# A graph attention layer on one core: the targets in 128 rows, the weights behind the first stores, and the one-hot in the middle of the step

## The chip, the cores and the metric

The kernel is one program on one core of a Trainium2 chip. The core has five instruction queues that run beside each other: TensorE (PE in the profile; matrix products and transposes, results into PSUM), VectorE (DVE), ScalarE (ACT), GpSimd (POOL, here only the indirect gathers) and SyncE (SP, which here issues nearly all other transfers). Each queue works in order. Transfers run on sixteen DMA engines. The metric is the device time of one execution in microseconds (us).

## The reference

There are 12,500 nodes with 128 values each and 400,000 edges, which are sorted by their target node `dst`; `src` is any node. H is 8 heads of 16 values.

```python
h = maximum(layernorm(x), 0)
message = (h @ w_src + b_src)[src] + (h @ w_dst)[dst]
rad_w = silu(silu(edge_attr @ fc_w1 + fc_b1) @ fc_w2 + fc_b2) @ fc_w3 + fc_b3
message = message * edge_weight * rad_w
message = message @ w_sep + b_sep            # per head: 16 for alpha, 16 values
alpha = smooth_leaky_relu(message_alpha)
score = sum over 16 of alpha * alpha_dot
att = softmax of score over the edges with the same dst
out = sum over the edges with the same dst of value * att
return x + out @ w_proj + b_proj
```

## The kernel before, in words

The program has four stages, and in all of them the order of each queue is the order in which the lines are written.

**The node stage** (L152 to L341). `x` is loaded in seven groups of 14 blocks of 128 nodes and a tail (L162, L163). A loop over 25 quads of four blocks computes: `stats` (L214, VectorE, every second quad for eight blocks, with one `rstd` on ScalarE), `norm` (L226, ScalarE), `turn` (L234, TensorE transposes, VectorE copies to `hT`) and `products` (L246): products with both node weights into PSUM, copies to `ms` (four buffers; ScalarE, in every fourth quad one of them VectorE) and two stores to the tables `t_src` and `t_dst` (L266) on SP. Before the loop SP is given, in this order: x, the targets `dst` as `cur` in 125 rows of 3200 (L169), the same shifted by one place as `prev` (L171, L172), each pair's first targets for the two halves of a pair as `base` (L176), the sections' first and last targets as `ends` (L177), and the block forms `w1b`, `w2b`, `w3b`, `b12` of the radial weights (L188 to L194). ScalarE's queue is given the two node weights (L159, L160) and fifteen weight loads (`load`, L108, L110). Eight completion counters are shared by the transfers of SP and ScalarE in turn, so a transfer is issued when the eighth before it has landed.

Two jobs sit in or behind the loop. `fits` (L271, after quad 12) counts places where `prev > cur` and sections whose targets span 64 nodes or more; the count `bad` decides later between the window form, which is taken with these inputs, and a general form. It also stores `ends` and loads them again, spread over the partitions, as `eb`. `cuts` (L303, after the loop) makes `sm`, which marks where a target changes (two passes over 3200 columns on VectorE), and stores it as `same`; it derives `w_score`, `w_s`, `v_out`, `b_s` and the window starts `far` and `tgt`.

**The edge stage** (`windows`, L656). 400 pairs of sections of 500 edges; step k of the loop at L1027 works on pair k, and with a lag of 12 on the sums of pair c = k - 12. `step` (L948) fixes the order of the queues. SP in a step: the stores of the last sums (`store_win` L920, `store` L924, the latter with a start read from `base`), the loads for pair k+3 (`load_w` L713, `load_md` L719, in every second step `load_d` L707), for k+6 (`load_e` L702), and now and then others (`prep_load`, `load_sm`, `load_x` L931, `zero` L136, scores out and back L836, L841, maxima L870). GpSimd gathers the source rows `gs` (L739). TensorE: third layer of the radial net (`mlp3`, L790), source rows and target rows into `pm` (L803, L811), first half of the values (`values(c, 0)`, L901), first `pa` (`alphas(k, 0)`, L820), `mlp1` of k+2, second half of the values, more source rows, second `pa`, `mlp2`, then `sums(c)` (L912), which multiplies the weighted values `pvx` by a one-hot matrix `oh` of the targets.

VectorE's order in a step: `sums_begin(c)` (L880) makes `oh` with two instructions (L888, L891) after ScalarE has copied the softmax weights into `pvx` (L884); then two `rad` (L794), two `mT` (L816), the first `pvx` (L903), `mr` (L728), the first `al` (L824), the second `pvx`, the second `al`, `ohT` (L783), `m` (L732). In each group of eight steps the softmax of the group before adds two scans (L852, L857), a difference (L862), an Exp and a transpose; in 25 of these groups `add_x` (L938) adds a bias to a loaded block of x, and every sixteenth step prepares indices (`prep_make`, L683). Twelve further steps (L1158) end the sums, beside jobs that combine sections which share a node. **The last stage** divides, multiplies by `w_proj` and adds x.

Of the kernel before, what the change touches and what calls it, by code (L numbers as in the profile page):

```python
# [21 lines left out]
F32 = mybir.dt.float32  # L22
BF16 = mybir.dt.bfloat16
I32 = mybir.dt.int32
AF = mybir.ActivationFunctionType
ALU = mybir.AluOpType
AX = mybir.AxisListType
# [3 lines left out]
P = 128  # L31
C = 128
H = 8
RAD = 32
BANK = 512
FC = 64
# [4 lines left out]
RP = 125  # L41
# [6 lines left out]
SEC = T * TS  # L48
# [8 lines left out]
def gnn_kernel(ctx: ExitStack, tc: tile.TileContext, a: dict, out: bass.AP):  # L57
    nc = tc.nc
    x, src, dst = a["x"], a["src"], a["dst"]
    ea, ew = a["edge_attr_32"], a["edge_weight1"]  # L60
    N, E = x.shape[0], src.shape[0]
    NB = -(-N // P)
    NT = E // P
    RC = E // RP
    NS = E // SEC
# [6 lines left out]
    const = ctx.enter_context(tc.tile_pool(name="const", bufs=1))  # L72
# [10 lines left out]
    same = dram.tile([1, E + 1], BF16, name="same")  # L83
# [21 lines left out]
    ident = const.tile([P, P], F32, name="ident")  # L105
    make_identity(nc, ident)

    def load(name, shape, ap=None, eng=None):  # L108
        t = const.tile(shape, F32, name="c_" + name)
        (eng or nc.scalar).dma_start(out=t, in_=a[name] if ap is None else ap)  # L110
        return t

    eps = const.tile([P, 1], F32, name="eps")
    nc.vector.memset(eps, LN_EPS)
    ones = const.tile([P, P], F32, name="ones")
# [14 lines left out]
    base = const.tile([1, 2, NP], I32, name="base")  # L130
# [23 lines left out]
    with tc.tile_pool(name="node", bufs=2) as np_, tc.tile_pool(name="node1", bufs=1) as n1, \  # L154
# [6 lines left out]
        for t0, t1 in groups:  # L161
            nc.sync.dma_start(out=x_all[:, t0:t1, :], in_=x_v[:, t0:t1, :])  # L162
        nc.sync.dma_start(out=x_all[:tail, NF, :], in_=x[NF * P:, :])  # L163
        dst_r = dst.rearrange("(p c) -> p c", p=RP)
        cur = n1.tile([RP, RC], I32, name="cur")
        prev = n1.tile([RP, RC], I32, name="prev")
        ends = n1.tile([100, 8, 2], I32, name="ends")
        eb = n1.tile([P, NS, 2], I32, name="eb")
        nc.sync.dma_start(out=cur, in_=dst_r)  # L169
        nc.vector.memset(prev[0:1, 0:1], -1)  # L170
        nc.sync.dma_start(out=prev[0:1, 1:RC], in_=dst_r[0:1, 0:RC - 1])  # L171
        nc.sync.dma_start(out=prev[1:RP, :], in_=dst[RC - 1:E - 1].rearrange("(p c) -> p c", c=RC))  # L172
        at = dst[0:1]
        with nc.allow_non_contiguous_dma(reason="the sections' ends"):
            for f in range(2):
                nc.sync.dma_start(out=base[:, f, :], in_=dst_h[f:f + 1, :, 0])  # L176
            nc.sync.dma_start(out=ends, in_=bass.AP(  # L177
                at.tensor, at.offset, [[8 * SEC, 100], [SEC, 8], [SEC - 1, 2]]))

        w1b = const.tile([P, P], F32, name="w1b")  # L180
        nc.vector.memset(w1b, 0.0)
        w2b = const.tile([P, P], F32, name="w2b")
        w3b = const.tile([P, C], F32, name="w3b")
        b12 = const.tile([P, 2], F32, name="b12")
        for f in range(2):
            for q in range(2):
                o = (2 * q + f) * RAD
                nc.sync.dma_start(out=w1b[o:o + RAD, f * FC:(f + 1) * FC], in_=a["fc_w1"])  # L188
            s = slice(f * FC, (f + 1) * FC)
            for q in range(2):  # L190
                nc.sync.dma_start(out=w2b[s, q * FC:(q + 1) * FC], in_=a["fc_w2"])
            nc.sync.dma_start(out=w3b[s, :], in_=a["fc_w3"])
            nc.sync.dma_start(out=b12[s, 0:1], in_=a["fc_b1"])
            nc.sync.dma_start(out=b12[s, 1:2], in_=a["fc_b2"])  # L194
        b_n = load("b_n", [C, 1], a["b_src"].rearrange("o c -> c o"))
        dot = load("dot", [C, 1])
        heads = load("heads", [C, C])
        w1, b1 = load("fc_w1", [RAD, FC]), load("fc_b1", [FC, 1])
        w2, b2 = load("fc_w2", [FC, FC]), load("fc_b2", [FC, 1])
        w3, b3 = load("fc_w3", [FC, C]), load("fc_b3", [C, 1])  # L200
        w_a, b_a = load("w_a", [C, C]), load("b_a", [C, 1])
        w_v = load("w_v", [C, C])
        w_proj = load("w_proj", [C, C])
        b_out = load("b_out", [P, C], a["b_proj"].to_broadcast([P, C]))
        b_v = load("b_v", [C, 1])


        mv = n1.tile([P, NB, 2], F32, name="mv")
# [60 lines left out]


        def fits():  # L271
            gt = n1.tile([RP, RC], BF16, name="gt")
            nc.vector.tensor_tensor(gt, prev, cur, op=ALU.is_gt)
            cnt = n1.tile([P, 2], F32, name="cnt")
            nc.vector.memset(cnt, 0.0)
            nc.vector.tensor_reduce(cnt[:RP, 0:1], gt, AX.X, ALU.add)
            span = n1.tile([100, 8], F32, name="span")
            nc.vector.tensor_sub(span, ends[:, :, 1], ends[:, :, 0])
            nc.vector.tensor_scalar(span, span, float(W - 1), None, op0=ALU.is_ge)
            nc.vector.tensor_reduce(cnt[:100, 1:2], span, AX.X, ALU.add)  # L280
            tot = nps.tile([1, 1], F32, name="tot", bufs=1)
            for j in range(2):
                nc.tensor.matmul(tot, cnt[:, j:j + 1], ones[:, 0:1], start=(j == 0), stop=(j == 1))
            nc.vector.tensor_copy(bad, tot)
            nc.sync.dma_start(out=ends_d[:, 1:2 * NS + 1].rearrange("o (p c) -> (o p) c", p=100),
                              in_=ends.rearrange("p s i -> p (s i)"))
            none = n1.tile([1, 2], I32, name="none")
            nc.vector.memset(none, -1)
            nc.sync.dma_start(out=ends_d[:, 0:1], in_=none[:, 0:1])
            nc.sync.dma_start(out=ends_d[:, 2 * NS + 1:2 * NS + 2], in_=none[:, 1:2])  # L290
            nc.sync.dma_start(out=t_dst[N:N + W, :], in_=z[:W, 0:C])
            nc.sync.dma_start(out=eb.rearrange("p s i -> p (s i)"),
                              in_=ends_d[0:1, 1:2 * NS + 1].to_broadcast([P, 2 * NS]))
# [7 lines left out]
        v_out = const.tile([P, C], F32, name="v_out")  # L301

        def cuts():  # L303
            sm = n1.tile([RP, RC], BF16, name="sm")
            nc.vector.tensor_tensor(sm, prev, cur, op=ALU.not_equal)
            nc.vector.tensor_scalar(sm, sm, RESTART, None, op0=ALU.mult)
            nc.sync.dma_start(out=same[:, 0:E].rearrange("o (p c) -> (o p) c", p=RP), in_=sm)
            nc.sync.dma_start(out=same[:, E:E + 1], in_=sm[0:1, 0:1])
            nc.vector.tensor_scalar(w_score, heads, dot, 0.8, op0=ALU.mult, op1=ALU.mult)
            nc.vector.memset(w_s, 0.0)  # L310
# [21 lines left out]
        for i in range(Q):  # L332
            if i % 2 == 0 and 4 * i + G < NB:
                stats(4 * i + G, min(4 * i + 2 * G, NB))
            if i + 2 < Q:
                norm(i + 2)
            if i + 1 < Q:
                turn(i + 1)
            products(i)
            if i == 12:  # L340
                fits()  # L341
        cuts()


    chunks = [(t, min(CH, TPI - t)) for t in range(0, TPI, CH)]
# [310 lines left out]
    def windows():  # L656
# [5 lines left out]
        with tc.tile_pool(name="wk2", bufs=2) as sp, tc.tile_pool(name="ps", bufs=1, space=PSUM) as pp, \  # L662
# [214 lines left out]
                nc.scalar.copy(Pem[m].rearrange("p t q h -> p t (q h)"), pt)  # L877


            def sums_begin(c):  # L880
                pvx[c] = sp.tile([T, 2, TS, ROW], F32, name="pvx")
                q = c % MP * 2
                for f in range(2):
                    nc.scalar.copy(pvx[c][:, f, :, C:ROW], Pem[c // MP][:, :, q + f, :])  # L884
                _, loc = prep[c // 16]
                ohs[c] = sp.tile([T, 8, W], F32, name="oh")
                t0 = c % 16 * 8
# [60 lines left out]
            def step(k):  # L948
# [28 lines left out]
                if has(k + 1):  # L977
                    split_md(k + 1, 0)
                if has(c):
                    sums_begin(c)  # L980
                rad = mlp3(k) if has(k) else None
                if has(k):
                    sources(k, 1)
# [13 lines left out]
                    mlp1(k + 2)  # L997
                if has(c):
                    values(c, 1)

                if has(k + 1):
                    sources(k + 1, 0)
# [323 lines left out]
```

## Time and profile before

| what | value |
|---|---|
| median of 3 runs | 4723.23 us (4720.04 to 4723.61) |
| the profiled execution | 4712.63 us, its span 4710.8 us |
| mean granted TensorE clock | 0.964 |
| busy PE / DVE / ACT / POOL | 4212.0 / 3081.2 / 1921.9 / 3136.0 us |
| node stage, until the edge stage's first load | 155.00 us |
| edge loop, about | 165 to 4505 us |
| last twelve steps, and last stage | to 4627, and to the end |

Line numbers (L820) are those of the kernel. In a timeline each line gives start, duration, engine (SPq and ACTq are the queues when they issue a transfer), line, operation, output and inputs, form and, in brackets, how long the engine had been idle and what ended that. A line of waits gives who waited for what: total us, times, longest. Every duration comes from one profiled execution; the sums of the prediction are made against it and then set beside the median.

### The profile page before, as it was taken

The numbers are of one execution on the slowest core, as the hardware profiler recorded it, in microseconds if no ns is written. First come the engines' busy times: TensorE is split into PE (matmuls) and PEld (weight loads), VectorE is DVE, ScalarE is ACT, GpSimd is POOL, SyncE is SP. The second block draws the span as 40 slices with busy tenths as digits, with TensorE's granted clock in tenths as the row PEclk, the third lists the DMA queues.
The fourth block names the chain that finished last, engine by engine and source line by source line (L and its number), as shares of the span: only waits on it lengthen the run. The fifth ranks groups of instructions, "written<-read, shape, count | busy, mean of one in ns | idle before, by whom it ended". The sixth has DMA issues, their size and how long they took to land.

```text
span 4710.8 us, 88096 instructions
## 1 busy us (share of the span) xinstructions
PE 4212.0 (89%) x29692; PEld 2344.1 (50%) x29692; DVE 3081.2 (65%) x6005; ACT 1921.9 (41%) x4595; POOL 3136.0 (67%) x3223
## 2 busy tenths in 40 slices
PE   4669998999999999999999999999999999999974
PEld 3325554554555555555545555555555555555553
DVE  4436665766766666666666666666666666666666
ACT  3324443443443444443433444444444444444421
POOL 0467776776777777777766777777777767777601
PEclk8779999999999999999999999999999999999987
DMA  4667767777776777777777777777677777777724
GB/s 160 168 162 173 175 167 172 174 178 175 170 176 171 169 176 175 172 178 174 170 175 170 177 174 169 179 172 164 171 174 169 171 168 170 172 168 174 173 64 173
DMA packets 901312, 796.36 MB, mean 169 GB/s; under 512 B 530125, under 2 KB 776829, under 8 KB 900598
## 3 DMA queue, kind: packets, MB, share of 16 engines
q1 hardware_dynamic: 794830, 573.36, 46.8%
q0 software_dynamic: 102816, 210.37, 21.5%
q10 hardware_dynamic: 3202, 6.92, 0.4%
q8 instruction: 234, 3.83, 0.4%
q14 instruction: 230, 1.88, 0.1%
HBM read 649.99 MB, written 140.67 MB: 168 GB/s over the span
## 4 chain that ended last, share of the span: by engine, by line
PE 66%; DVE 10%; DMA 9%; SPq 6%; ACT 5%; issue 4%; POOL 1%; ACTq 0%; POOLq 0%; DVEq 0%
PE pa L820 14%; PE V L901 13%; PE misc L912 7%; PE p L790 6%; PE pm L803 6%; PE pm L811 4%; PE p L758 4%; PE misc L831 4%; PE p L773 4%; DMA md<-t_dst 2%; DMA sc_d<-Sp 2%; PE m L749 2%; ACT sl L822 2%; DMA agg<-ob 2%; DVE al L824 2%
## 5 line engine op out<-in xcount | busy, mean ns | idle before, releaser
L739 POOL DMA_INDIRECT gs<-t_src,idx x3200 | 3121.6, 976 | 1347.2 <-issue 800.8
L822 ACT ACTIVATE sl<-pa,c_b_a 128x500 f32<-128x500 f32 x800 | 541.4, 677 | 1595.5 <-PE pa L820 1594.7
L824 DVE SCALAR_TENSOR_TENSOR al<-pa,sl 128x500 f32<-128x500 f32 x800 | 543.1, 679 | 828.8 <-ACT sl L822 723.6
L820 PE MATMUL pa<-mT,c_w_a 128*128 128x500 f32 x1600 | 851.2, 614 | 244.2 <-DVE mT L816 173.3
L901 PE MATMUL V<-c_w_v,mT 128*125 128x128 f32 x6208 | 895.5, 288 | 0.3
L901 PEld LDWEIGHTS V<-c_w_v,mT 128*125 128x125 f32 x6208 | 746.4, 190 | 290.7 <-issue 176.8
L794 DVE SCALAR_TENSOR_TENSOR rad<-p,c_fc_b,w_b 128x500 f32<-128x500 f32 x800 | 552.9, 733 | 307.2 <-PE p L790 305.7
L903 DVE TENSOR_TENSOR pvx<-V,Pem 125x512 f32<-125x512 f32 x776 | 531.9, 685 | 114.4 <-PE V L901 107.8
L816 DVE SCALAR_TENSOR_TENSOR mT<-pm,c_b_n,rad 128x500 f32<-128x500 f32 x800 | 552.5, 733 | 6.5 <-PE pm L811 6.5
L803 PEld LDWEIGHTS pm<-ident,gs 125*128 125x128 f32 x3200 | 356.7, 142 | 312.8 <-issue 292.3
L803 PE MATMUL pm<-ident,gs 125*128 125x125 f32 x3200 | 505.0, 280 | 7.9 <-DMA gs<-t_src,idx 7.9
L912 PE MATMUL misc<-pvx,oh 125*64 125x136 f32 x6400 | 470.1, 288 | 31.4 <-DVE pvx L903 27.6
L912 PEld LDWEIGHTS misc<-pvx,oh 125*64 125x64 f32 x6400 | 364.5, 138 | 182.9 <-issue 178.6
L790 PE MATMUL p<-h,w3b 64*128 64x500 f32 x1600 | 446.0, 634 | 2.4 <-ACT h L776 2.4
L820 PEld LDWEIGHTS pa<-mT,c_w_a 128*128 128x128 f32 x1600 | 245.0, 193 | 284.5 <-DVE mT L816 195.4
L811 PE MATMUL pm<-ohT,m 64*128 64x500 bf16 x2400 | 323.9, 376 | 0.0
L758 PE MATMUL p<-eT,w1b 64*128 64x250 f32 x1600 | 287.5, 437 | 1.0 <-ACT eT L751 1.0
L725 ACT CAST m<-md 128x128 bf16<-128x128 f32 x400 | 118.3, 296 | 401.1 <-DMA md<-t_dst 400.8
L758 PEld LDWEIGHTS p<-eT,w1b 64*128 64x128 f32 x1600 | 124.7, 191 | 307.5 <-issue 276.3
L761 ACT ACTIVATE h<-p,b 128x500 f32<-128x500 f32 x400 | 272.4, 681 | 4.8 <-PE p L758 4.8
L776 ACT ACTIVATE h<-p,b 128x500 f32<-128x500 f32 x400 | 269.2, 673 | 3.6 <-PE p L773 3.6
L888 DVE TENSOR_TENSOR oh<-lane,loc 125x504 f32<-125x504 f32 x400 | 269.2, 673 | 0.0
(145 smaller groups left out, 3286.1 us busy)
## 6 DMA issues: line engine op xcount, KB each, us to landing
w_b<-in_edge_weight SPq DMA_DIRECT2D x400, 500.0 KB
d_b<-in_dst SPq DMA_DIRECT2D x400, 250.0 KB
gs<-t_src,idx POOLq DMA_INDIRECT x3200
e_t<-in_edge_attr SPq DMA_DIRECT2D x400, 125.0 KB
sc_d<-Sp SPq DMA_DIRECT2D x200, 250.0 KB
win<-ob SPq DMA_DIRECT2D x400, 68.0 KB
agg<-ob SPq DMA_DIRECT2D x800, 33.5 KB
md<-t_dst SPq DMA_DIRECT2D x800, 32.0 KB
```

The lines of the kernel that those rows point to most:

```text
L739: nc.gpsimd.indirect_dma_start(out=gs[:, j, :], out_offset=None, in_=t_src[:, :], in_offset=bass.IndirectOffsetOnAxis(ap=idx[:, t:t + 1], ...
L758: nc.tensor.matmul(p1[:, q, 0:2 * T], w1b[s, :], eTs[k][s, :], start=True, stop=True)
L790: nc.tensor.matmul(p3[:, f, 0:SEC], w3b[s, :], h2s[k][s, :], start=True, stop=True)
L794: nc.vector.scalar_tensor_tensor(rad[:, s], p3[:, f, 0:SEC], b3, w_g[k][:, s], op0=ALU.add, op1=ALU.mult)
L803: nc.tensor.matmul(pms[k, f][:, t * T:(t + 1) * T], gs[:T, t, :], ident[:T, :T], start=(t == 0), stop=False, is_transpose=True, skip_group ...
L816: nc.vector.scalar_tensor_tensor(mTs[k][:, s], pm[f], b_n, rad[:, s], op0=ALU.add, op1=ALU.mult)
L820: nc.tensor.matmul(pa, w_a, mTs[k][:, f * SEC:(f + 1) * SEC], start=True, stop=True)
L822: nc.scalar.activation(sl, pa, AF.Silu, bias=b_a, scale=1.0)
L824: nc.vector.scalar_tensor_tensor(al, pa, 0.25, sl, op0=ALU.mult, op1=ALU.add)
L901: nc.tensor.matmul(V[:, t, :], mTs[c][:, o:o + T], w_v, start=True, stop=True)
L903: nc.vector.tensor_mul(pvx[c][:, f, :, 0:C].rearrange("p t (h k) -> p t h k", h=H), V.rearrange("p t (h k) -> p t h k", h=H), Pem[c // MP] ...
L912: nc.tensor.matmul(acc[f * W:(f + 1) * W, :], ohs[c][:, f * TS + t, :], pvx[c][:, f, t, :], start=(t == 0), stop=(t == TS - 1), skip_group ...
```

## The change

The separate loads on ScalarE's queue go. All weights and the targets are asked for on SP, after the stores of the second quad's products: first the targets, then the fifteen weights, then the block forms w1b, w2b, w3b and b12 in the order of before. The targets come once, as 128 rows of 3125 with one more column in front, whose value is the last target of the row before: `cur[:, 1:]` is what `cur` was, `cur[:, :-1]` what `prev` was. `cuts` runs after quad 20, inside the loop. In the edge stage `sums_begin` is cut in two: `weights(c)` stays at its place, and `one_hot(c)` is called after the second half of the values. All else is as before.

```diff
-    def load(name, shape, ap=None, eng=None):
-        t = const.tile(shape, F32, name="c_" + name)
-        (eng or nc.scalar).dma_start(out=t, in_=a[name] if ap is None else ap)
-        return t
...
-        nc.sync.dma_start(out=cur, in_=dst_r)
-        nc.vector.memset(prev[0:1, 0:1], -1)
-        nc.sync.dma_start(out=prev[0:1, 1:RC], in_=dst_r[0:1, 0:RC - 1])
-        nc.sync.dma_start(out=prev[1:RP, :], in_=dst[RC - 1:E - 1].rearrange("(p c) -> p c", c=RC))
...
+        CC = E // P
+        cur = n1.tile([P, CC + 1], I32, name="cur")
+        nc.vector.memset(cur[0:1, 0:1], -1)
...
+        wt = {name: const.tile(shape, F32, name="c_" + name) for name, shape in (
+            ("b_src", [C, 1]), ("dot", [C, 1]), ("heads", [C, C]), ("fc_w1", [RAD, FC]), ("fc_b1", [FC, 1]),
+            ("fc_w2", [FC, FC]), ("fc_b2", [FC, 1]), ("fc_w3", [FC, C]), ("fc_b3", [C, 1]), ("w_a", [C, C]),
+            ("b_a", [C, 1]), ("w_v", [C, C]), ("w_proj", [C, C]), ("b_proj", [P, C]), ("b_v", [C, 1]))}
...
+        def load_targets():
+            nc.sync.dma_start(out=cur[:, 1:CC + 1], in_=dst.rearrange("(p c) -> p c", p=P))
+            at = dst[CC - 1:CC]
+            with nc.allow_non_contiguous_dma(reason="single targets"):
+                nc.sync.dma_start(out=cur[1:P, 0:1], in_=bass.AP(at.tensor, at.offset, [[CC, P - 1], [1, 1]]))
+                for f in range(2):
+                    nc.sync.dma_start(out=base[:, f, :], in_=dst_h[f:f + 1, :, 0])
+                at = dst[0:1]
+                nc.sync.dma_start(out=ends, in_=bass.AP(
+                    at.tensor, at.offset, [[8 * SEC, 100], [SEC, 8], [SEC - 1, 2]]))
+
+        def load_weights():
+            for name, t in wt.items():
+                ap = a[name]
...
+                nc.sync.dma_start(out=t, in_=ap)
+            for f in range(2):
...
...
-            nc.vector.tensor_tensor(gt, prev, cur, op=ALU.is_gt)
+            nc.vector.tensor_tensor(gt, cur[:, 0:CC], cur[:, 1:CC + 1], op=ALU.is_gt)
...
-            nc.vector.tensor_tensor(sm, prev, cur, op=ALU.not_equal)
+            nc.vector.tensor_tensor(sm, cur[:, 0:CC], cur[:, 1:CC + 1], op=ALU.not_equal)
...
             products(i)
+            if i == 1:
+                load_targets()
+                load_weights()
             if i == 12:
                 fits()
-        cuts()
+            if i == 20:
+                cuts()
...
-            def sums_begin(c):
+            def weights(c):
                 pvx[c] = sp.tile([T, 2, TS, ROW], F32, name="pvx")
                 q = c % MP * 2
                 for f in range(2):
                     nc.scalar.copy(pvx[c][:, f, :, C:ROW], Pem[c // MP][:, :, q + f, :])
+
+            def one_hot(c):
                 _, loc = prep[c // 16]
                 ohs[c] = sp.tile([T, 8, W], F32, name="oh")
...
                 if has(c):
-                    sums_begin(c)
+                    weights(c)
...
                 if has(c):
                     values(c, 1)
+                    one_hot(c)
```

## The prediction

> **What bounds the kernel now.** I read the chain of waits first, then the waits in total, then the timeline of the start, of the end of the node stage and of steady steps, and last the SP queue's own waits.
>
> ```profile
> PE 66%; DVE 10%; DMA 9%; SPq 6%; ACT 5%; issue 4%; POOL 1%; ACTq 0%; POOLq 0%; DVEq 0%
> ```
>
> By the chain this looks like a TensorE kernel. It is one only inside a step. The start (all times in us from the span's start, columns start and duration):
>
> ```profile
> 14.53 1.28 ACT L221 ACT_TABLE_LOAD   x1 [14.53 <-DMA c_b_a<-in_b_a]
> 15.83 0.30 ACT L221 ACTIVATE rstd<-mv,eps 128x4 f32<-128x4 f32 x1
> ...
> 19.81 13.10 SPq L176 DMA_DIRECT2D base<-in_dst  x2
> 32.95 13.82 SPq L177 DMA_DIRECT2D ends<-in_dst  x1
> 46.89 15.71 SPq L188 DMA_DIRECT2D w1b<-in_fc_w  x2
> ...
> 70.05 0.52 SPq L266 DMA_DIRECT2D t_src<-ms  x1
> 73.29 0.58 ACT L261 COPY ms<-pm 128x512 f32<-128x512 f32 x1 [34.57 <-DMA t_dst<-ms]
> ```
>
> Two delays stand here. ScalarE cannot begin before 14.53, because its own queue issues fifteen weight loads until 14.50; the statistics of the first four blocks were ready at 7.79 (first BN_STATS 6.10, last aggregate 7.61 and 0.18). And the SP queue stands in three issues from 19.81 to 62, so the first store of node products leaves at 70.05; the four `ms` buffers are full, and ScalarE waits 34.57. What the queue stands behind is in the stretches (last two columns: share of the 16 DMA engines, GB/s):
>
> ```profile
> 20.00:25.00 5.00, 4.89 (x14) 3.24 (x14) 4.07 (x18) 2.40 (x7) 0.00 (x0) 1.00 1.01 422
> 30.00:35.00 5.00, 3.96 (x18) 2.84 (x19) 3.26 (x14) 4.73 (x12) 0.00 (x0) 1.00 0.34 123
> 50.00:55.00 5.00, 0.00 (x0) 0.00 (x0) 0.00 (x0) 0.00 (x0) 0.00 (x0) 0.50 0.24 85
> ```
>
> While x arrives all engines work; once only `cur` (125 rows) and `prev` (124) are left, a third to a quarter of them do. The node stage ends so:
>
> ```profile
> 142.19 3.48 DVE L305 TENSOR_TENSOR sm<-prev,cur 125x3200 bf16<-125x3200 int32 x1
> 147.07 0.28 SPq L307 DMA_DIRECT2D same<-sm  x1
> 155.00 0.36 SPq L674 DMA_DIRECT2D ri<-in_src  x1
> ```
>
> In the edge steps, one in eight looks like this:
>
> ```profile
> 2322.59 1.19 DVE L857 TENSOR_TENSOR_SCAN M<-sm,M 128x500 f32<-128x500 bf16 x1
> 2324.41 0.68 DVE L888 TENSOR_TENSOR oh<-lane,loc 125x504 f32<-125x504 f32 x1
> 2325.01 0.17 DVE L891 TENSOR_TENSOR oh<-loc,far 125x8 f32<-125x8 f32 x1
> 2325.09 1.38 DVE L794 SCALAR_TENSOR_TENSOR rad<-p,c_fc_b,w_b 128x500 f32<-128x500 f32 x2
> 2327.16 1.11 PE L820 MATMUL pa<-mT,c_w_a 128*128 128x500 f32 x2 [1.12 <-DVE mT L816]
> ```
>
> The scan makes VectorE late, the one-hot (L888, L891) stands before `rad`, and TensorE waits 1.12. But who paces the steps? The waits in total (us, times, longest):
>
> ```profile
> ACT m L725 <- DMA md<-t_dst: 400.8, 133, 10.6
> PE pa L820 <- DVE mT L816: 173.3, 93, 10.0
> DVE xs L938 <- DMA xs<-in_x: 74.9, 17, 9.7
> ```
>
> ```profile
> SPq L924 <- DMA agg<-ob: 150.8, 230, 7.8
> SPq L841 <- DMA sc_d<-Sp: 139.8, 49, 9.2
> ```
>
> The engines wait for what SP asked for late, while SP waits for its own transfers. I matched SP's issues with what they need, between 200 and 4480: each store of sums (L920) starts at least 2.5 after the copy (L916) that feeds it, median 12.1; each L836 at least 1.4 after its L834; each `w_b` load 11.4 or more after its buffer was last read. So SP never waits for a compute engine there; its issues follow each other without end. `md` is cast within 3.2 of its issue, with ScalarE idle, in 74 steps, the last at step 395 of 400. **The SP queue sets the length of the edge loop**; TensorE catches up with it and waits.
>
> **The change, part by part.**
>
> *ScalarE's queue loses the weight loads.* Only the two `w_nodes` remain, so the first `rstd` comes at 7.79 and some 0.06 instead of 15.83: 8.0 earlier, and all that follows it, up to the second products. x is no obstacle: it drains at 422 GB/s, and its second group is due only at 19.39 - 8.0 = 11.4.
>
> *The SP hold.* In the order of before without a stall, the second products are copied until 28.07; their two stores take to 29.05, now 21.05. Then the queue holds for a time H: five target loads, 29 weight loads. Those fifteen from ScalarE: 0.33 to 0.69 each in the trace with the gaps, without waits 8.2. The fourteen block loads: 62.19 to 69.94 for thirteen, so 8.3. The targets: `cur` 0.3, its transfer 1.6 MB at 422 GB/s is 3.8, behind half a MB of stores (1.3). The 127-row column has no row in the trace. Against the row of 128 single words that does stand there (`rb`, L680: issue 0.64, read 1.83 after it) it would cost 0.6. The Trainium skill, "DMA: Bandwidth & Descriptors", section "Why a DMA increments its semaphore by 16 and not by 1", speaks for one half of this edit and against the other: a transfer uses the largest number of engines up to 16 that divides its slow dimension, so 125 rows 5, 124 rows 4, 128 rows 16, but 127 rows one. The 0.34 and 0.24 above agree with 5 and 4 of 16 (0.31, 0.25). By it all 127 words queue on one engine behind its part of `cur`, and the two `base` loads cannot be accepted until most of them are taken, as L176 and L177 were not. I take this: 5.1 for `cur` and the stores, 1 for the column, 2 for `base` and `ends` (1600 words). That is 8.1; by the `rb` row alone it would be some 3, and as long as in before (2.5 + 10.5 + 13.8 of issue) 27. H = 8.1 + 8.2 + 8.3 = 24.6, bounds 19 and 43.
>
> Behind the hold stand the stores of products 2 to 5. `ms` has four buffers, so products 6 are the first to wait. Stores to the copy took 3.25 in before (70.05 to 73.29, rounded): the copy comes at 21.05 + 24.6 + 3.25 = 48.9. In before the copies of products 6 came at 80.21, and 74.8 later, at 155.00, the edge stage began. So 123.7, less 0.15 as the two passes of `fits` (3.48 and 3.49) shrink by 75 of 3200 columns.
>
> *The cuts in the middle.* Before, their VectorE work ran from 142.19 to 150.53, with `same` landing at 154.86 as the last thing (125 rows). The node stores alone had landed by 148.4 (the next stage's waits for them pass then), so 6.4 goes. But some 7.9 of VectorE work (the 8.3, less the shorter rows and part of a wait of 0.89 for TensorE) now stand ahead of the transposed copies of quad 22. The nearest row is `fits`, alike in form: with 7.8 of VectorE work the `rstd` that should come 6.81 after 98.25 came 14.57 after, 7.76 lost. Cost 7.8 - 6.4 = +1.4. If TensorE covers none of the gap before hT (0.96), less; bounds 0 and +3.5. In the upper one stands the scaling of `sm` (0.99 for 3200, a quarter of the 3.48 that one element per clock takes): rows are now 3125 long. By the row it is 0.97; one per clock would be 3.4. The Trainium skill, "VectorE: DVE Perf Modes", section "Walkthrough: the 8-slice pipeline in each mode", allows the fast form for an odd dimension if source and destination are equal, as they are here; no row shows it. I take 0.97. The two `same` issues cost SP 0.6 between stores, which then wait for VectorE anyway.
>
> Edge stage from 125.0 instead of 155.0: **-30**. GpSimd's gathers start with it and keep their distance; nothing is moved past its queue.
>
> *The one-hot.* Moved behind the second value product, before the second `al`. There VectorE waits 1.35 for ScalarE in an ordinary step (2018.47), the pair takes 0.60 and 0.17: hidden, and `oh` ends 1.36 after the second `pvx` begins (2006.10), 2007.46, before the sums begin at 2007.84. If the cover were gone, 388 x 0.77 = 299. At the old place it frees 0.68 in the steps where VectorE is late: over all steps, the smaller of what `rad` could come earlier and of TensorE's wait before `pa` adds up to 54. That is TensorE's time, not SP's: SP issues exactly as before, so what TensorE gains there it waits for `md` and `xs` later. Value 0 to -54; I take -0.5, what is left after step 395. In the twelve last steps nothing lies between pvx and the sums: three of them run TensorE, VectorE, TensorE in turn and get 0.95 each, the rest are held by other VectorE work or transfers: +3 (0 to +6).
>
> Sum: -30 + 3 - 0.5 = -27.5. The profiled run took 4712.6 around a span of 4710.8; the median of the runs is 4723.2. 4723.2 - 27.5 = **4696**.
>
> **The rivals.**
> *TensorE is the bound after all* (chain: 66%): the 54 arrive too, 4642. For it: TensorE is busy 4021 of 4340 in the loop. Against it: SP's issues never waited for it. 0.13, parts of it included.
> *The queue holds on as before*: the column on one engine blocks, H = 43, a stall of 30 instead of 11.5: 4715. For it: three issues of 10 to 15 in before. Against: those stood behind 33 us of transfers on 5 engines. 0.15.
> *Slower: the sums wait for the one-hot.* At L912, 16 matmuls in every step. The margin is 0.38; TensorE has some 0.7 per step to spare against SP (199 of idle on `md`, 75 on `xs`, over 400). So it decides from 1.1 late, and each 0.1 beyond costs 39: 1.25 late gives 4762. Against it: VectorE's idle time is there in nearly all steps (721 waits before `al`). 0.09.
>
> **How the numbers follow.** Forecast 0.63, with its own range 4684 to 4707 from the bounds of H, cuts and tail. The range 4650 to 4718 takes in parts of the first rival and most of the second; it leaves out about 0.2. A measurement of this kernel tells 0.2% (9.4) from nothing. Faster, below 4714: the forecast, the first rival and some of the second, 0.82; same 0.08; slower 0.10, the third rival and rest.
>
> **What would show it.** First `rstd` near 7.9; `cur` landing within 8 of its issue, the column's followers short; first store of products 2 near 46; edge stage from 125; one-hot without TensorE waiting at L912 in the loop; TensorE's wait for mT down by about 50 and ScalarE's wait for `md` up by the same; the loop from first to last step as long as before. Wrong would be a loop shorter by tens of us (SP not the pacer), or a hold over 40.

## The result, and the profile after

The changed kernel takes 4686.7 us (median of 5 runs, 4672.0 to 4692.86) where the kernel before takes 4721.15 (5 runs, 4716.71 to 4723.61): ratio 0.9923, 95% interval 0.9905 to 0.9941, so 28 to 45 us faster. On a second chip, in the run e9_changed below, it is 4601.4 against 4628.78: 0.9941, interval 0.9927 to 0.9956. Ratios and intervals leave out executions more than 1.5% above the fastest of the same kernel; only e12 had any (two of six). The two profiled executions differ by 25.9, and this is where:

| stretch of the profiled execution, us | before | after | difference |
|---|---|---|---|
| start, to the edge stage's first load | 155.00 | 123.00 | -32.00 |
| from there to the first `al` | 22.51 | 25.07 | +2.55 |
| edge loop, first `al` of its first step to first `al` of its last | 4331.48 | 4333.26 | +1.78 |
| from there to the end | 201.77 | 203.59 | +1.82 |
| span | 4710.77 | 4684.91 | -25.85 |

All the gain lies ahead of the edge stage; 2.55 of it is lost again on the way to the first `al`. The runs of one kernel lie up to 21 us apart, so the small differences behind it say no more than "unchanged".

The chain of waits on the page of the changed kernel (shares of the span by engine):

```profile
PE 62%; DMA 10%; DVE 9%; SPq 8%; ACT 5%; issue 4%; POOL 1%; ACTq 0%; POOLq 0%; DVEq 0%
```

Next to the line of before, TensorE's share is 4 points lower, and transfers and the SP queue together hold 18% (before 15%).

The start, from the timeline of the changed kernel (start, duration, engine, line):

```profile
7.90 0.30 ACT L221 ACTIVATE rstd<-mv,eps 128x4 f32<-128x4 f32 x1 [4.94 <-DVE mv L219]
...
21.02 0.45 SPq L178 DMA_DIRECT2D cur<-in_dst  x1
21.52 0.31 SPq L181 DMA_DIRECT2D cur<-in_dst  x1
21.88 6.66 SPq L183 DMA_DIRECT2D base<-in_dst  x2
28.58 0.92 SPq L185 DMA_DIRECT2D ends<-in_dst  x1
29.55 1.40 SPq L195 DMA_DIRECT2D c_b_src<-in_b_src  x1
...
38.97 0.89 SPq L199 DMA_DIRECT2D w1b<-in_fc_w  x2
...
47.21 0.51 SPq L266 DMA_DIRECT2D t_src<-ms  x1
...
50.44 1.07 ACT L261 COPY ms<-pm 128x512 f32<-128x512 f32 x2 [12.84 <-DMA t_dst<-ms]
```

The first `rstd` no longer waits for ScalarE's queue. SP holds the node stores from 21.02 to 47.21: 8.5 us for the targets, 9.4 for the fifteen weights, 8.2 for the block forms. In the targets one issue stands out: the first of the two `base` loads is held for 6.01, right behind the column of 127 single words (L181), which itself was accepted in 0.31. The packets in the trace show what it stands behind: the rows of `cur` (12,500 bytes each) move from 22.56 to 28.15, and the 127 words of the column only from 27.68 to 28.45; the `base` load is accepted at 27.89. So most of the 6.01 is the transfer of `cur` itself. The four buffers of `ms` leave 12.84 of ScalarE's time uncovered.

The end of the node stage:

```profile
105.09 3.41 DVE L305 TENSOR_TENSOR sm<-cur 128x3125 bf16<-128x3125 int32 x1
108.53 0.98 DVE L306 TENSOR_SCALAR sm<-sm 128x3125 bf16<-128x3125 bf16 x1
109.54 0.34 SPq L307 DMA_DIRECT2D same<-sm  x1
...
113.39 0.69 DVE L243 COPY hT<-pt 128x512 f32<-128x512 f32 x1
...
117.80 0.38 DVE L243 COPY hT<-pt 128x212 f32<-128x212 f32 x1 [0.76 <-PE pt L240]
...
123.00 0.34 SPq L678 DMA_DIRECT2D ri<-in_src  x1
```

`same` is stored while node products are still being made, and the first load of the edge stage follows the last node store (issued until 122.85) at once.

In the edge loop, the step that the prediction showed (the second scan stands in it):

```profile
2295.77 0.67 DVE L894 TENSOR_TENSOR oh<-lane,loc 125x504 f32<-125x504 f32 x1
2296.36 0.17 DVE L897 TENSOR_TENSOR oh<-loc,far 125x8 f32<-125x8 f32 x1
2296.91 1.15 PE L918 MATMUL misc<-pvx,oh 125*64 125x136 f32 x16
...
2298.39 1.19 DVE L861 TENSOR_TENSOR_SCAN M<-sm,M 128x500 f32<-128x500 bf16 x1
...
2300.22 1.38 DVE L798 SCALAR_TENSOR_TENSOR rad<-p,c_fc_b,w_b 128x500 f32<-128x500 f32 x2
...
2302.29 1.11 PE L824 MATMUL pa<-mT,c_w_a 128*128 128x500 f32 x2 [0.45 <-DVE mT L820]
```

The one-hot now comes before the scan instead of behind it, and TensorE waits 0.45 before `pa` where it waited 1.12. And the waits in total, of the engines and of the SP queue:

```profile
ACT m L729 <- DMA md<-t_dst: 485.0, 147, 11.0
PE pa L824 <- DVE mT L820: 149.4, 98, 10.2
DVE xs L944 <- DMA xs<-in_x: 98.4, 21, 10.3
```

```profile
SPq L930 <- DMA agg<-ob: 157.5, 236, 6.1
SPq L845 <- DMA sc_d<-Sp: 135.5, 50, 9.8
```

SP's waits for its own transfers (150.8 and 139.8 before) hardly changed. TensorE's wait for `mT` fell by 24, ScalarE's wait for `md` rose by 84 and VectorE's for `xs` by 24. What the loop was given at one place it lost at another. The length of a step, by its place in a group of eight (mean from the first `al` of a step to that of the next, steps 16 to 388; place 2 holds the second scan):

| place | 0 | 1 | 2 | 3 | 4 | 5 | 6 | 7 | sum |
|---|---|---|---|---|---|---|---|---|---|
| before | 9.26 | 10.97 | 12.09 | 11.33 | 9.27 | 10.64 | 11.36 | 11.39 | 86.31 |
| after | 9.25 | 11.06 | 11.26 | 11.33 | 9.32 | 10.71 | 11.76 | 11.72 | 86.41 |

Place 2 is 0.83 shorter, about the price of the one-hot; places 6 and 7 are 0.40 and 0.33 longer. TensorE's idle time goes the same way: from 1.19 to 0.50 at place 2, from 1.77 to 1.99 at place 6 and from 0.50 to 0.73 at place 7. At places 0, 4 and 5 it is under 0.1 before and after, so these steps are filled by TensorE's own work.

### The profile page after: what moved, and what is told of

Its sections match the earlier page's. It is cut to its first block, busy times and chain, and to the rows that moved or that the text cites. A ratio compares the mean times of both kernels' runs of the same rounds, so it can differ in the third digit from the quotient of the medians.

```text
span 4684.9 us, 88079 instructions
## 1 busy us (share of the span) xinstructions
PE 4218.8 (90%) x29692; PEld 2346.5 (50%) x29692; DVE 3081.3 (66%) x6005; ACT 1920.9 (41%) x4595; POOL 3126.9 (67%) x3223
## 4 chain that ended last, share of the span: by engine, by line
PE 62%; DMA 10%; DVE 9%; SPq 8%; ACT 5%; issue 4%; POOL 1%; ACTq 0%; POOLq 0%; DVEq 0%
PE pa L824 13%; PE V L907 12%; PE misc L918 6%; PE p L794 6%; PE pm L807 6%; PE pm L815 4%; PE misc L835 4%; PE p L762 4%; PE p L777 3%; DMA agg<-ob 3%; DMA md<-t_dst 2%; DMA sc_d<-Sp 2%; SPq L930 2%; ACT sl L826 2%; PE m L753 2%
## 5 line engine op out<-in xcount | busy, mean ns | idle before, releaser
L820 DVE SCALAR_TENSOR_TENSOR mT<-pm,c_b_src,rad 128x500 f32<-128x500 f32 x800 | 552.6, 732 | 2.6 <-PE pm L815 2.6
L918 PEld LDWEIGHTS misc<-pvx,oh 125*64 125x64 f32 x6400 | 362.8, 138 | 186.1 <-DVE oh L897 140.5
L729 ACT CAST m<-md 128x128 bf16<-128x128 f32 x400 | 118.3, 296 | 485.2 <-DMA md<-t_dst 485.0
## 6 DMA issues: line engine op xcount, KB each, us to landing
e_t<-in_edge_attr SPq DMA_DIRECT2D x400, 125.0 KB
```

The costliest lines, as they stand in the source:

```text
L820: nc.vector.scalar_tensor_tensor(mTs[k][:, s], pm[f], b_n, rad[:, s], op0=ALU.add, op1=ALU.mult)
L918: nc.tensor.matmul(acc[f * W:(f + 1) * W, :], ohs[c][:, f * TS + t, :], pvx[c][:, f, t, :], start=(t == 0), stop=(t == TS - 1), skip_group ...
```

## The experiments

The runs fell into five groups, each on one chip. The time of the kernel before differs between them, so each run is compared with the kernel before in its own group only:

| chip | its number | kernel before, us | its mean granted TensorE clock | runs |
|---|---|---|---|---|
| A | not noted | 4721 | 0.964 | the prediction's two kernels |
| B | 1 | 6149 | 0.877 | e1 to e4 |
| C | 15 | 4629 | 0.969 | e9 to e11 |
| D | 13 | 6018 | 0.879 | e12 |
| E | 8 | 6178 | 0.873 | e5 to e8 |

A's number was not noted, and each of the others was met once, so it isn't shown whether a chip is always slow or only at times.

**One half at a time (chip B).** Theory: SP paces the loop, so the one-hot's move is worth nothing and the loads are worth the start. First the move alone, in the kernel before:

```diff
-                    sums_begin(c)
+                    weights(c)
...
                     values(c, 1)
+                    one_hot(c)
```

> The kernel before with the one-hot alone moved behind the second value product. SP paces the loop (theory of the prediction): the loop from first to last step keeps its length, time within 6 us of before; TensorE's wait for mT falls and ScalarE's wait for md rises. TensorE paces (rival): 25 to 54 us faster than before. Sums wait for the one-hot (rival): slower by more than 10 us.

Measured: 5909.2 us against 6149.32, ratio 0.962 (0.9573 to 0.9667): neither 0 nor 25 to 54 us faster, but 240. None of the three cases held. The other half, the changed kernel with the one-hot back at its old place:

```diff
                     weights(c)
+                    one_hot(c)
...
                     values(c, 1)
-                    one_hot(c)
```

> The changed kernel with the one-hot back at its old place, ahead of rad: only the loads, the targets in 128 rows and the cuts remain changed. SP paces: the edge stage starts at 123 as in the changed kernel, and the time is within 6 us of it (about 4685). TensorE paces: 25 to 54 us slower than the changed kernel, so about as slow as before. Sums wait: faster than the changed kernel by some 5 to 20 us.

Measured: 6096.44, ratio 0.9915 (0.9879 to 0.995); the edge stage starts at 121.87. So on this chip the halves have changed roles: the loads bring 0.9%, the one-hot 4%. What is different here is in the timeline of e2_loads_only:

```profile
2311.73 1.14 PE L907 MATMUL V<-c_w_v,mT 128*125 128x128 f32 x8
...
2313.96 1.10 PE L824 MATMUL pa<-mT,c_w_a 128*128 128x500 f32 x2 [1.09 <-issue]
...
2319.81 0.69 DVE L909 TENSOR_TENSOR pvx<-V,Pem 125x512 f32<-125x512 f32 x1 [5.26 <-remote]
2319.89 1.28 ACT L826 ACT_TABLE_LOAD   x1 [7.26 <-remote]
...
2320.55 2.07 PE L907 MATMUL V<-c_w_v,mT 128*125 128x128 f32 x8 [4.87 <-DVE pvx L909]
```

The products V are recorded as done at 2312.9, and VectorE, idle, begins to read them at 2319.81; "remote" means that no recorded instruction released it. ScalarE, which is to read `pa` (recorded as done at 2315.06), goes on at 2319.89. So both readers of TensorE's results are released at nearly the same moment, long after the recorded ends. These ends are modelled, so the profile can't tell a late message from matmuls that really ended later. TensorE then waits 4.87, and the same eight matmuls take 2.07 instead of 1.14. The stretches around it (busy time of PE, PEld, DVE, ACT, POOL, then granted clock, DMA share, GB/s):

```profile
2312.00:2316.00 4.00, 2.60 (x14) 1.28 (x13) 2.55 (x4) 0.64 (x4) 3.08 (x4) 1.00 0.87 49
2316.00:2320.00 4.00, 0.00 (x0) 0.00 (x0) 0.19 (x1) 0.11 (x1) 1.40 (x2) 0.82 0.77 168
2320.00:2324.00 4.00, 3.44 (x13) 3.04 (x14) 2.07 (x4) 2.62 (x4) 0.27 (x1) 0.50 0.85 195
```

First the results are late, at full clock; then TensorE, idle, is set to half clock. The second is what the Trainium skill, "TensorE: Matmul & The Clock Gate", section "Part 1: The HAM clock gate (the "warmup" mystery)", states: idle for a window of some 3.4 us halves the clock; in this trace 242 of the 247 half-clock stretches last 3.4, 6.8 or 10.2. For the first no run here shows a cause. Between 500 and 4000 us, VectorE begins a reading of V more than 1.2 us after both the last recorded matmul of V and its own last instruction in 31% of the cases here and in 30% in e1_onehot_only. In the kernel before and the changed kernel on chip A, and in the changed kernel on chip C, it does so in none of some 650 each. With that, SP is no longer the one that is late:

```profile
SPq L840 <- ACT m L729: 1255.4, 167, 11.3
```

On chip A, SP's wait at this line (L840, the stores of the scores) for ScalarE was 20 (10.9 and 9.1). ScalarE's wait for `md`, 485 on chip A, is 9.3 here. So on chip B, by these waits, the steps are set by late results on the way from TensorE over VectorE and ScalarE and back. TensorE's waits with the one-hot at its old place (e2_loads_only):

```profile
PE pa L824 <- DVE mT L820: 340.7, 151, 25.5
PE V L907 <- DVE pvx L909: 262.9, 78, 5.0
```

and at its new place (e1_onehot_only):

```profile
PE pa L820 <- DVE mT L816: 271.1, 183, 4.5
PE V L903 <- DVE pvx L905: 145.2, 49, 5.6
PE misc L914 <- DVE oh L893: 133.0, 92, 8.8
```

The loop from first to last `al` is 5771 in the one and 5495 in the other, 276 apart; TensorE's busy time for the same matmuls, over the whole execution, is 4740.4 and 4587.1, 153 apart, with a mean clock of 0.878 in one and 0.896 in the other. More than half of the loss in these two executions is thus slower matmuls, the rest idle time. (The profiled execution of e2_loads_only, 6149.29, is the slowest of its twelve and 53 above their median. From the medians, with the later start of e1_onehot_only taken off, 28.8 at the first `al`, the loss is 216.)

**The one-hot alone, once more.** The same kernel a second time:

> The same kernel as in the run with the one-hot alone moved, asked for a second time: there the kernel before itself took 6149 at a granted clock of 0.88, and the move was worth 4%. Theory: it is worth its whole price (388 x 0.6 to 0.77, 230 to 300 us) where TensorE, held back by its clock, sets the steps, and nothing where the SP queue does. If the kernel before takes about 4720 here (clock 0.96): within 6 us of it. If it takes about 6150 (0.88): 3.5 to 4.3% faster again. The rival, that the move is worth tens of us on any chip: 25 to 54 us faster at 0.96 too.

Measured: on another slow chip, E, before 6178.35, this 5908.88, ratio 0.9556 (0.9517 to 0.9594). It repeats.

**Relief for SP (e3 and e4 on chip B, e8 on chip E).** The loads of edge attributes go to ScalarE's queue, in the changed kernel and with the one-hot at its old place:

```diff
-                nc.sync.dma_start(out=e_g[k], in_=ea_t[k])
+                nc.scalar.dma_start(out=e_g[k], in_=ea_t[k])
```

> The changed kernel with the 400 loads of edge attributes asked for by ScalarE instead of SP, nothing else. SP paces by its own issues: each step frees SP of 0.48 us of issue and of some 1.1 us for which the issue behind it is held, up to 1.5 us of 10.86; TensorE is 94% busy in the loop, so it takes over after 0.5 us or so a step: 100 to 220 us faster, 4470 to 4590, with ScalarE's wait for md far under 485 us. If it is not SP's issues but the transfers or TensorE that pace the loop: within 20 us of the changed kernel.

> As the run with the edge attributes on ScalarE, with the one-hot at its old place. If SP paced before and TensorE paces once SP is relieved: 20 to 54 us slower than that run, because now TensorE's wait for mT counts. If SP still paces: within 6 us of it. If the sums' wait for the one-hot costs more than the earlier rad brings: faster than that run.

> The changed kernel with the loads of edge attributes on ScalarE's queue, a second time. At a clock of 0.96, where SP paces: 100 to 220 us faster than the changed kernel, ScalarE's wait for md well under 485. At 0.88, where TensorE paces, it was worth only some 30 us over the one-hot's move, with the loads' 26 among them. If the loop at 0.96 is paced by the transfers themselves or by TensorE: within 20 us of the changed kernel.

Measured: e3 5879.43, 0.9572 (0.9523 to 0.9622); e4 6096.1, 0.9919 (0.9887 to 0.9952); e8 5899.17, 0.9552 (0.9506 to 0.9598). With the one-hot at its old place the relief changes nothing (0.9919 against 0.9915 on the same chip). That fits a loop that SP doesn't pace there, but it says nothing about the chip of the prediction. The changed kernel itself was not run on chip B or E, so what the relief does with the one-hot at its new place is not measured there.

**Twice the one-hot (chip E).** Both instructions are issued a second time at the new place, in the changed kernel:

```diff
                     values(c, 1)
                     one_hot(c)   # within it, each of the two tensor_tensor now stands twice
```

> The changed kernel with both one-hot instructions issued a second time at their new place, so that the sums' one-hot is ready 0.77 us later in each of 388 steps. SP paces: the prediction's margin of 0.38 and TensorE's spare 0.7 a step take it up but for some 0.1: 0 to 40 us slower than the changed kernel, and TensorE's wait for oh at the sums grows from 37 to some 250 us while ScalarE's wait for md shrinks by about as much. TensorE paces: each step is 0.7 longer, 250 to 300 us slower.

Measured: 5899.0, ratio 0.9557 (0.9509 to 0.9606), level with e8 on the same chip. TensorE's waits:

```profile
PE misc L925 <- DVE oh L904: 380.0, 208, 9.9
PE pa L824 <- DVE mT L820: 144.1, 79, 26.4
...
PE V L914 <- DVE pvx L916: 44.2, 19, 5.6
```

and with a single one-hot at the new place on the same chip (e6_weights_spread, below):

```profile
PE pa L830 <- DVE mT L826: 318.6, 197, 29.7
PE V L913 <- DVE pvx L915: 137.2, 46, 5.4
PE misc L924 <- DVE oh L903: 129.9, 87, 9.3
```

The sums now wait 380 for the one-hot, 250 more, and the two other waits are together 268 smaller. The loop is 5472, with a single one-hot 5495 (e6) and 5539 (e5). VectorE is busy 281 us more (3367.4 against 3086.4 in e6), and the loop is no longer for it; the steps behind it, from the last step's first `al` to the end of the sums, take 109.25 instead of 94.45. So the simple form "TensorE paces, each 0.77 counts" fell too. What costs on these chips is not the work but its old place, between the product of the radial net and `rad`. Why just there was not settled.

**The hold (chip E).** In the changed kernel the 29 weight loads no longer go out in one piece:

```diff
             if i == 1:
                 load_targets()
-                load_weights()
+            if 2 <= i < 12:
+                for load in loads[3 * (i - 2):3 * (i - 1)]:
+                    load()
```

(`loads` holds the same 29 transfers in the same order.)

> The changed kernel with its 29 weight loads no longer in one piece behind the first node stores but three behind the stores of each of quads 2 to 11. The hold of the SP queue then is that of the targets alone, 8.5 us, under the 13.1 that four buffers of node products cover: ScalarE's wait for ms goes, and the edge stage starts at 110 instead of 123. If the hold was not what set the node stage (rival: x, the statistics, or the targets): it starts at 120 to 123. The edge loop is unchanged: 13 us faster than the changed kernel in all (at 0.96).

Measured: 5867.08, ratio 0.9499 (0.9459 to 0.9539). The SP queue at the start and at the edge stage:

```profile
21.50 6.08 SPq L183 DMA_DIRECT2D base<-in_dst  x2
27.63 0.91 SPq L185 DMA_DIRECT2D ends<-in_dst  x1
28.65 1.30 SPq L270 DMA_DIRECT2D t_src<-ms  x1
...
110.57 0.34 SPq L684 DMA_DIRECT2D ri<-in_src  x1
```

The edge stage starts at 110.57 as worked out, and ScalarE's wait for `ms` is gone from the waits of the start. In the changed kernel it starts at 122.69 and 123.00 (chips C and A), and at 123.16 in e7 on this chip: 12.6 us for nothing but a different spacing. The 29 loads were what held the node stage; the targets' 8.5 are covered by the four buffers. Not all of it reaches the edge loop: the first `al` comes at 171.10, in e7 at 178.81, 7.7 later. On chip E it is the fastest of the runs (0.9499 against 0.9552 to 0.9557, with intervals that overlap). On chips A and C it was not run, so what it is worth to the whole kernel there is not measured.

**The changed kernel on another fast chip.**

> The changed kernel itself, beside the kernel before on the chip of these runs. If the chip is the one on which the kernel before takes 6150 to 6180: the one-hot's move (0.9556 and 0.962 of before) and the rest (0.9915) together, 0.948 to 0.954, some 290 us faster; the edge stage from 123. If it is one on which before takes 4720: 0.992 again.

Measured: the runs fell on chip C, before 4628.78, this 4601.4, ratio 0.9941 (0.9927 to 0.9956). The edge stage starts at 122.69. The even steps last 9.27 as on chip A, the loop is 4252, 81 shorter than on chip A, and ScalarE waits 117 less for what SP asked for:

```profile
ACT m L729 <- DMA md<-t_dst: 367.8, 133, 12.3
```

(485.0 on chip A.) That fits a loop which SP and its transfers pace, but doesn't prove it.

**SP as the pacer by force (chip C).** The kernel before, and the kernel before with the one-hot moved, each with the edge attributes of a step loaded five times into the same buffer, each load waiting for the one before it to land:

```diff
-                nc.sync.dma_start(out=e_g[k], in_=ea_t[k])
+                for _ in range(5):
+                    nc.sync.dma_start(out=e_g[k], in_=ea_t[k])
```

> The kernel before with the load of edge attributes issued five times in each step into the same buffer, so that SP's queue is made longer by four loads (1.5 us each at least) and paces the steps on any chip: 17 us a step or more, 6800 to 9000. ScalarE's wait for md, 9 to 400 us before, becomes thousands. It is the partner of the next run.

> As the run with five loads of edge attributes in a step, with the one-hot behind the second value product. Theory: what the move is worth depends on who paces the steps; with SP made the pacer it is worth nothing, so within 0.4% of that run, also on a chip where alone it brought 4%. Rival, that the move shortens every step by what TensorE is spared, whoever paces: 3 to 4% faster than that run.

Measured: 9748.8 (9743.36 to 9755.35) and 9745.86 (9741.95 to 9759.26), against the kernel before 2.1058 (2.1026 to 2.109) and 2.1063 (2.1031 to 2.1096). The SP queue's and the engines' waits of e10_five_et_loads:

```profile
SPq L703 <- DMA e_t<-in_edge_attr: 5336.1, 1594, 8.0
```

```profile
ACT m L726 <- DMA md<-t_dst: 1607.6, 350, 21.6
```

The queue waits 3.3 for each repeated load, the steps are 23.3 long (in all more than the 6800 to 9000 expected), and the move is worth nothing, where on chips B and E it is worth 4%. The mean clock of these two is 0.721 and 0.722, lower than on chips B and E: so a low clock alone doesn't make the move pay.

**Both, on a third slow chip.** The weights spread, and the edge attributes on ScalarE's queue:

> The changed kernel with the 29 weight loads spread behind quads 2 to 11 and the loads of edge attributes asked for by ScalarE. The first edit ends before the edge stage and is read there: it starts at 110 instead of 123. The second is read in the loop, from the first al to the last. SP paces the loop by its own issues (where the kernel before takes 4630 to 4720, ScalarE's wait for md near 400): SP is relieved of up to 1.5 us of 10.7 in each step, and TensorE, whose work alone is 9.27 in an even step and 10.33 in an odd one, sets the pace: loop 80 to 250 us shorter than the changed kernel's 4252 to 4333, wait for md under 200. The loop is paced by the transfers or by TensorE already: within 20 us of it, and 13 us faster than the changed kernel in all. On the chip where before takes 6150: about as the run with the weights spread (0.950).

Measured: chip D, before 6018.38, this 5877.67, ratio 0.968 (0.9623 to 0.9736). The edge stage starts at 110.99, the spreading holds on a further chip. In the loop the late results of chips B and E are here too (22% of the readings of V begin over 1.2 us late, counted as above). So the question for which it was made, whether SP's relief shortens the loop where `md` is late, was not answered. It stays open.

## Why the prediction was right

**The whole.** 4696 was forecast, 27.5 less than before; measured were 34.5 less in the medians, 25.9 in the profiled pair and 27.4 on chip C. The chain of reasons held: the start carries the gain, the loop none. That the sum came so near is in part luck: the edge stage began 2.0 earlier than forecast, and 2.55 was lost between its first load and the first `al`, for which the forecast had no term.

**First `rstd`** at 7.90; 7.85 was worked out.

**The hold.** 26.2 for 24.6: targets 8.5 for 8.1, fifteen loads 9.4 for 8.2 (two of them took 1.40 and 1.06), fourteen block loads 8.2 for 8.3. Within the targets the shares were about right too. The rows of `cur` landed 7.1 after their issue (counted: 5.1, and 0.3 of issue), the 127 words took 0.77 (counted: 1), `base` and `ends` after the first acceptance 1.6 (counted: 2). The row of `rb`, which would have given 3 for the targets, was the wrong guide. The rule that the prediction cites from the Trainium skill, "DMA: Bandwidth & Descriptors", section "Why a DMA increments its semaphore by 16 and not by 1", fits: in the trace 144 packets of four bytes go from 26.71 to 28.45, the 127 words and 17 more. Each of the node stores ahead, which go over 16 engines by that rule, is followed by 16 such packets; so 16 of the 17 belong to `cur` and one to the column, as if one engine had carried it. Whether the `base` load would have been accepted sooner without the column was not run. Products 6 were copied at 50.44 for 48.9, and ScalarE waited 12.84 for 11.5. That these 29 loads, not the targets, overfill the buffers was shown by e6.

**The cuts** are the step that failed, in both its terms, though the errors are small: +1.4 was forecast, with bounds 0 and +3.5, and it was -2.0. The VectorE work in the middle cost 5.9 and not 7.8 (from the copy of `ms` at 134.50 before, 104.49 after, to the last copy of `hT`: 7.40 and 13.31). The work itself is 8.3 long, from 105.09 to 113.39. But VectorE had stood idle in this stretch anyway, 4.25 in all (0.96 before the copy of `hT` at 136.14, and the two waits of before shown here), of which 1.83 is left after:

```profile
139.99 0.17 DVE L222 RECIPROCAL rstd<-rstd 128x2 f32<-128x2 f32 x1 [2.35 <-ACT rstd L221]
...
141.90 0.38 DVE L243 COPY hT<-pt 128x212 f32<-128x212 f32 x1 [0.94 <-PE pt L240]
```

```profile
116.08 0.17 DVE L222 RECIPROCAL rstd<-rstd 128x2 f32<-128x2 f32 x1 [1.07 <-ACT rstd L221]
```

(The other wait of after, 0.76, is in the lines above.) The prediction took its size from `fits`, where nearly all of the work had cost time, and of this idle time it had only the 0.96 in its bounds. And moving `same` away gave 7.9 and not 6.4 (from the last copy of `hT` to the first edge load: 13.10 and 5.20), because that load does not wait for the node stores to land: it is issued at 123.00, when SP has issued the last of them until 122.85. I had read a wait for their landing from the waits at 148.4. So the edge stage starts at 123.0 and not 125.0, although the hold was 1.6 longer. The scaling of `sm` at 3125 columns took 0.98, as the row said, and as the rule on odd dimensions allows that the prediction cites from the Trainium skill, "VectorE: DVE Perf Modes", section "Walkthrough: the 8-slice pipeline in each mode"; the pass that makes `sm` took 3.41.

**The one-hot.** Its result, nothing on this chip, came as said: loop +1.78, place 2 of the group shorter by about the pair's price. It is given back at places 6 and 7: VectorE's wait for `xs` grew by 0.51 in each group (place 6), ScalarE's for `md` by 0.47 and 0.16. The move alone was not run on a fast chip, so this rests on the two profiled executions. Two sizes were off. TensorE's wait for `mT` fell by 24 and not by 50. And the margin of 0.38 at the sums was not there. Their first weight load waits for `oh` in 375 steps, 0.37 each. But TensorE's idle time before the sums, now put down to `oh`, hardly grew:

```profile
L912 PE MATMUL misc<-pvx,oh 125*64 125x136 f32 x6400 | 470.1, 288 | 31.4 <-DVE pvx L903 27.6
```

```profile
L918 PE MATMUL misc<-pvx,oh 125*64 125x136 f32 x6400 | 465.4, 288 | 37.3 <-DVE oh L897 37.3
```

(The first is before, the second after. The idle time ahead of the weight loads there, which run beside earlier matmuls, went from 182.9 to 186.1: before, nothing that the profile shows ended it.) So the one-hot is now what comes last before the sums, as the third rival has it, but it costs some 6 us of TensorE's time in all.

**"The SP queue sets the length of the edge loop"** is right in what it predicted and too simple as a sentence. On chips A and C the ordinary even step lasts 9.27, which is TensorE's work back to back (in the changed kernel's step from 1362.57 to 1371.84 its groups of matmuls follow each other without a gap). Between the recorded matmuls from 200 to 4380 it is idle for 304 us before and 291 after; what is freed at one wait returns as another, because the transfers asked for by SP come no earlier. Shown is that a loop that SP, waiting for its transfers, paces by force swallows the move whole (e10, e11). That SP does the same in the untouched kernel rests on the waits of three traces, not on an experiment: the runs that were to show it (e3, e8, e12) fell on chips where SP is not late. Nor do the traces part SP's own issues from the transfers that hold them up.

**The rivals.** TensorE as the bound, 4642: not on A and C. The hold as long as before, 4715: no, 26 for 43. Slower by the sums' wait: no. (Its own figures, 39 for each 0.1 beyond 1.1, give 4754 and not 4762 for 1.25.) That the one-hot could be worth 240 us where TensorE's results come late was in none of the cases; on chips B and E the forecast's -27.5 would have been far off (0.962 and 0.9556 for the one-hot's move alone), for a reason that the trace of chip A could not show. The forecast holds for chips A and C; that the result was taken on a fast one was luck.

**The last twelve steps**, +3 forecast: from the first `al` of the last step to the end of the sums it took 94.36 before and 95.38 after, +1.

## What to carry to other kernels

A burst of small loads in front of stores costs what the buffers behind it don't cover: count the hold against the buffers' cover, and spread the loads over the iterations (here the same 29 transfers then let the edge stage begin 12 us earlier, of which 7.7 were left at its first `al`). An edit that frees an engine inside a loop is worth only what the loop's latest resource lets through: sum the waits by place before and after, and expect them to move rather than vanish. And if an operation has two legal places, take the one that does not stand between a result of TensorE and the instruction that TensorE waits for next: on chip A nothing of it could be seen, on two slow chips it was worth 4%.

## What the runs showed of the hardware

- The same kernel took 4629, 4721, 6018, 6149 and 6178 us in five groups of runs on chips A to E. On B, D and E VectorE begins to read TensorE's results up to 6 us after the recorded end of the matmuls, and over 1.2 us after it in 22 to 32% of the readings of V, although the program runs on one core only; in the profiled executions of the kernel before and the changed kernel on A and C never more than 1.12. What holds them back no profile here shows.
- 127 single words asked for behind a transfer of 1.6 MB were accepted in 0.31. They moved only as that transfer ended, and the next issue on the queue was held for 6.01 (chip A; 5.58 in e9 on chip C).
- An elementwise pass over 3125 columns of bf16 took 0.98 with an odd row length, 3200 columns 0.99.
- A further load of the same 1000 pieces of 128 bytes into the same buffer cost SP 3.3 us of waiting.
